# Gram stages of a two-block bottleneck network: other pixels in the first transfer step, normalisation traced step by step, issues split nine to seven

## The chip, the core and the metric

The kernel runs on one core of a Trainium2 chip, in float32. The metric is the time of one launch in device microseconds. The core has five engines that run side by side, each with its own queue of instructions, worked in order: TensorE (PE in the profile, with its weight loads as PEld), VectorE (DVE), ScalarE (ACT), GpSimd (POOL) and SyncE (SP), which here only issues transfers. Engines wait for each other through semaphores. Sixteen DMA engines move data, and a transfer is issued from the queue of one engine; in this kernel from SP, POOL and ACT.

## The reference, cut to what matters

Two residual bottleneck blocks, one after the other, each with batch normalisation over all 64 x 14 x 14 = 12,544 pixels:

```python
# x: (64, 1024, 14, 14)
out = relu(bn(conv(x, w1, b1, 1, 0), g1, be1))      # 1024 -> 256, 1x1
out = relu(bn(conv(out, w2, b2, 1, 1), g2, be2))    # 256 -> 256, 3x3
out = bn(conv(out, w3, b3, 1, 0), g3, be3)          # 256 -> 1024, 1x1
out = softplus(residual_scale)[0] * out
return relu(x + out)
# bn: (x - mean) * rsqrt(var + 1e-5), mean and var over images and pixels of each channel
```

## The kernel before

All 256 channels of the middle layer stay in on-chip memory as `y_all`: 128 partitions (channels), two halves (`MS` = 2), 12,544 pixels (`NPX`). The first convolution is fused with the last one of the block ahead; the 3x3 convolution (`conv2`) runs in a Winograd form with the products on TensorE; the last convolution is folded with its normalisation and the residual addition.

The third batch normalisation needs mean and variance of the last convolution's output before that output exists. They follow from the Gram matrix of the normalised middle activations: the sum over pixels of y yᵀ (256 x 256) and of y. Computing it is the **Gram stage** (`gram`, L904), once in each block. It goes so:

- Each piece of `y_all` is normalised in place by ScalarE (`norm`, L536, scale, shift and ReLU in one activation) and then has a constant subtracted by VectorE (`less`, L1233). Pieces are listed in `bounds`: pixels 0 to 256, to 768, to 1568, and then every 1568 (`GPX`). Both halves of each piece: 20 normalisations and 20 subtractions.
- TensorE contracts over its partitions, so pixels must lie on partitions: y has to be transposed, 256 pixels (`CH` x `P`) at a time. There are 49 such pairs of chunks. A transposed pair goes to one of six buffers `zt`, and four products (two into `g0`, two into `g1`; L169, outputs `cp` and `ap`) take it up.
- Seven of the 49 pairs are transposed by TensorE itself (`by_tensor`, L936) and copied by VectorE to `zt` (L942): the first six (`FIRST`), and the last one.
- The other 42 go through VectorE (`by_vector`, L948), whose transposition works on 32 x 32 squares. For that the squares must first be moved across partitions, by DMA: `spread(k)` (L922) moves one step of 1536 pixels (`STEP`) from `y_all` to a tile `x`, in sixteen transfers of 96 KB (L928), four by four groups of 32 partitions. There are seven steps of six pairs, with two tiles in turn (`homes`; in block 0 the first is the memory of `ws`, so the profile says `ws` and `home`; in block 1 both are `home`). Step k+2 overwrites the tile of step k, so it is issued when step k's six transpositions are done.
- The sixteen transfers of a step are issued by two queues, ten by SP and six by POOL.

Products are issued one pair behind the transpositions. After the last pair come the statistics (`conv3_stats`) and the rest of the block.

A scheduler orders the instructions of each engine when the kernel is built: it takes what was traced and picks by readiness and priority, except where `keep_in_program_order` fixes it (transpositions and products are fixed; normalisations, subtractions and copies are not). The order is then static: an engine's instruction waits for whatever stands ahead of it on that engine.

In the kernel before, all pieces are normalised and subtracted first in the trace; then two steps are spread, then the loop over pairs runs and spreads step k+2 after step k's six pairs. TensorE's first six pairs take pixels 0 to 1535; the steps take 1536 to 12,287; the last pair 12,288 to 12,543.

Of the kernel before, what the change touches and what calls it, by code (L numbers as in the profile page):

```python
# [41 lines left out]
P = 128  # L42
# [4 lines left out]
MS = M // P  # L47
# [5 lines left out]
NPX = N * HW  # L53
CH = 2
NZT = 6

FIRST, LAST = 6, 1
RUN = 3 * P
STEP = 4 * RUN
# [7 lines left out]
GPX = GI * HW  # L67
# [24 lines left out]
def bottlenecks(ctx: ExitStack, tc: tile.TileContext, x, w1s, w2s, w3s, pars, out):  # L92
    nc = tc.nc
# [5 lines left out]
    y_all = keep.tile([P, MS, NPX], FP, tag="y", name="y")  # L99
# [67 lines left out]
    def matmul(*args, **kw):  # L167

        tc.keep_in_program_order(nc.tensor.matmul(*args, **kw))  # L169
# [155 lines left out]
    def act(*args, **kw):  # L325

        tc.keep_in_program_order(nc.scalar.activation(*args, **kw))  # L327
# [205 lines left out]
    def norm(s, y, aff, act=nc.scalar.activation):  # L533

        scale, shift = aff
        act(y, y, AF.Relu, bias=shift[:, s : s + 1], scale=scale[:, s : s + 1])  # L536
# [367 lines left out]
    def gram(psum, pool, homes, aff, less, beside):  # L904

        g0, g1 = psum.tile(M + 1, "cp"), psum.tile(P + 1, "ap")
        zts = [pool.tile([P, CH, M + 1], FP, tag=f"zt{i}", name=f"zt{i}") for i in range(NZT)]
        for zt in zts:  # L910
            nc.gpsimd.memset(zt[:, :, M:], 1.0)
        zts = itertools.cycle(zts)
        start = FIRST * CH * P

        bounds = [0, CH * P, 3 * CH * P, *range(GPX, NPX + 1, GPX)]
        for a, e in zip(bounds, bounds[1:]):
            for s in range(MS):
                y = y_all[:, s, a:e]
                norm(s, y, aff)
                less(s, y)  # L920

        def spread(k):  # L922

            x = homes[k % 2][:, : MS * STEP].rearrange("p (s j f) -> p s j f", s=MS, j=4)
            for i, j in itertools.product(range(4), range(4)):
                queue = nc.gpsimd if (4 * i + j) % 8 in (2, 5, 7) else nc.sync
                a = start + k * STEP + i * RUN
                queue.dma_start(out=x[32 * i : 32 * i + 32, :, j], in_=y_all[32 * j : 32 * j + 32, :, a : a + RUN])  # L928
            return x.rearrange("p s j f -> p (s j) f")

        def by_tensor(a):
            tp = psum.tile(CH * M)
            for c in range(CH):
                for s in range(MS):
                    tc.keep_in_program_order(
                        nc.tensor.transpose(  # L936
                            tp[:, (c * MS + s) * P : (c * MS + s + 1) * P],
                            y_all[:, s, a + c * P : a + (c + 1) * P], ident,
                        )
                    )  # L940
            zt = next(zts)
            nc.vector.tensor_copy(zt[:, :, :M], tp.rearrange("p (c m) -> p c m", c=CH))  # L942
            return zt

        def by_vector(x, i):
            zt = next(zts)
            tc.keep_in_program_order(
                nc.vector.transpose(  # L948
                    zt[:, :, :M].rearrange("p b (n c) -> p b n c", c=32),
                    x[:, :, i * CH * 32 : (i + 1) * CH * 32].rearrange("p n (b r) -> p b n r", r=32),  # L950
                )
            )
            return zt

        def pairs():
            for i in range(FIRST):
                yield by_tensor(i * CH * P)
            for k in range(STEPS):
                x = ready.pop(0)
                for i in range(RUN // (CH * 32)):  # L960
                    yield by_vector(x, i)
                if k + 2 < STEPS:
                    ready.append(spread(k + 2))
            for i in range(LAST):
                yield by_tensor(NPX - (LAST - i) * CH * P)

        ready = [spread(k) for k in range(2)]
        total = NPX // (CH * P)
        before = None
        for k, zt in enumerate(itertools.chain(pairs(), (None,))):  # L970
            if before is not None:
                for c in range(CH):
                    first, last = k == 1 and c == 0, k == total and c == CH - 1
                    matmul(g0, before[:, c, 0:P], before[:, c, :], start=first, stop=last)
                    matmul(g1, before[:, c, P:M], before[:, c, P:], start=first, stop=last)
            before = zt
            if k in beside:
                beside[k]()
        return g0, g1
# [126 lines left out]
    def aggregate(stats, first):  # L1106
        n = stats.shape[1]
        mv = small.tile([P, n, nc.vector.BN_AGGR_DIM], FP, tag=f"mv{n}", name="mv")
        for o in range(n):
            nc.vector.bn_aggr(mv[:, o, :], stats[:, o, first:, :].rearrange("p t f -> p (t f)"))  # L1110
        return mv

    def affine(mv, n, par, g, be, conv_bias=None):

        def tl(name):
            return small.tile([P, n], FP, tag=f"{name}{n}", name=name)

        v, sd, r, q = tl("v"), tl("sd"), tl("r"), tl("q")  # L1120
        nc.scalar.activation(sd, mv[:, :, 1], AF.Sqrt, bias=eps)
        nc.vector.tensor_scalar(v, mv[:, :, 1], EPS, None, ALU.add)
        nc.vector.reciprocal(r, sd)

        nc.vector.tensor_mul(q, r, v)
        nc.vector.scalar_tensor_tensor(q, q, -0.5, r, ALU.mult, ALU.mult)
        nc.vector.scalar_tensor_tensor(r, q, 1.5, r, ALU.add, ALU.mult)
        scale, shift = tl("scale"), tl("shift")
        nc.vector.tensor_mul(scale, r, par[:, g : g + n])
        if conv_bias is None:  # L1130
            off = mv[:, :, 0]
        else:

            off = tl("off")
            bias = par[:, conv_bias : conv_bias + n]
            nc.vector.tensor_add(off, mv[:, :, 0], bias)
            nc.vector.tensor_sub(off, off, bias)
        nc.vector.scalar_tensor_tensor(shift, off, -1.0, scale, ALU.mult, ALU.mult)
        nc.vector.tensor_add(shift, shift, par[:, be : be + n])
        return scale, shift  # L1140
# [33 lines left out]
    with tc.tile_pool(name="first", bufs=1) as one, tc.tile_pool(  # L1174
# [17 lines left out]
        pieces = list(itertools.product(range(2), range(MS), range(MS)))  # L1192
# [16 lines left out]
    for b in range(2):  # L1209
# [4 lines left out]
        aff = affine(aggregate(stats1, T - 3 + b), MS, pb, G1, BE1)  # L1214
# [4 lines left out]
        with tc.tile_pool(name=f"last_{b}", bufs=1) as one, tc.tile_pool(  # L1219
# [5 lines left out]
            aff = affine(aggregate(stats2, 0), MS, pb, G2, BE2)  # L1225
            with ExitStack() as scope:
# [4 lines left out]
                with tc.tile_pool(name=f"gram_{b}", bufs=1) as pool:  # L1231
                    def less(k, y):
                        nc.vector.tensor_scalar(y, y, minus_c[:, k : k + 1], None, ALU.add)  # L1233

                    def x_tile(name):
                        return xpool.tile([P, CS * PX], FP, tag="x", name=name)


                    ws = sums_tile(one, 2 - b)
                    homes = [x_tile("home") if b else ws.rearrange("p i n -> p (i n)"), x_tile("home")]  # L1240

                    weights = []

                    def combined():
                        if b == 0:
                            weights.append(combine_w1(w1, ws[:, 1]))
                        weights.append(combine_w3(w3, ws[:, 0]))

                    beside = {FIRST + STEPS * RUN // (CH * 32): combined}
                    grams = gram(psum, pool, homes, aff, less, beside)  # L1250

                    made = [conv3(psum, 0, o, w3, "cx" if b else "ay") for o in range(2)]
                    mv3 = small.tile([P, CS, nc.vector.BN_AGGR_DIM], FP, tag="mv3", name="mv3")
                    conv3_stats(psum, pool, grams, w3, mv3, ("cy", "cp", "cy", "cp" if b else "cx"))
                aff = affine(mv3, CS, pb, G3, BE3, conv_bias=B3)
# [50 lines left out]
```

## Time and profile before

| | us |
|---|---|
| median of seven runs | 2016.35 (2015.07 to 2018.89) |
| the profiled execution: its time / its span | 2015.07 / 2013.1 |
| block 0, first normalisation of the Gram stage starts | 603.98 |
| block 0, first VectorE transposition starts | 626.90 |
| block 0, TensorE's first products for the statistics, behind the Gram products | 690.25 |
| block 1, first normalisation starts | 1597.51 |
| block 1, first VectorE transposition starts | 1620.34 |
| granted TensorE clock, mean over the span | 0.985 |

One profiled execution lies behind the profile; its time includes some 2 us that are not in the span. A line of the waits reads: engine, line, what it waited for, then total us, times, longest. A line of the timeline reads: start, us, engine, line, operation, output and input with shapes, how many, and in brackets the idle time before with what ended it. A line of windows reads: stretch, its length, then busy us (and instructions) of PE, PEld, DVE, ACT and POOL, the granted TensorE clock as a share of full speed, the DMA engines' share and GB/s. For a group of instructions: busy us and mean ns of one behind the bar.

### The profile page before, as it was taken

Reading aid. Unit: us, or ns where it says so; the run is one execution under the profiler, and the core shown is the slowest. Engines: PE = TensorE matmul, PEld = TensorE weight load, DVE = VectorE, ACT = ScalarE, POOL = GpSimd, SP = SyncE. Lnnn points to the kernel's source line nnn. Section 1 sums busy time; section 2 is a strip of 40 time slices with the busy share of each in tenths; the row PEclk is TensorE's granted clock in tenths of the full one; section 3 lists DMA queues with packets and bytes.
Section 4 is the critical chain, followed back from the end, with each engine's and each line's share of the span. In section 5 each row is a group of like instructions: output and inputs, shape, how many; then the busy total and the mean of one; then the engine's idle time right before and its main releaser. Section 6 shows DMA issues by size and latency. Waiting matters only on the chain.

```text
span 2013.1 us, 27547 instructions
## 1 busy us (share of the span) xinstructions
PE 1947.4 (97%) x9560; PEld 1641.1 (82%) x9560; DVE 1586.8 (79%) x2844; ACT 940.5 (47%) x1915; POOL 617.0 (31%) x676
## 2 busy tenths in 40 slices
PE   8999999999987999999999999999999888999999
PEld 4555558999987889999999999899999876555554
DVE  5788758999986566777777677699999864899897
ACT  1222214466645055555555555445566521556555
POOL 0111101121213134333333433211221140666665
PEclk9999999999998999999999999999999898999999
DMA  7866625555546534444444444256656384799998
GB/s 269 291 249 248 247 97 175 181 191 186 190 136 179 199 128 161 176 178 166 187 161 184 169 170 183 96 181 191 194 184 193 100 203 172 259 327 334 329 338 299
DMA packets 176218, 407.63 MB, mean 202 GB/s; under 512 B 12368, under 2 KB 143504, under 8 KB 159568
## 3 DMA queue, kind: packets, MB, share of 16 engines
q1 hardware_dynamic: 162208, 330.44, 48.1%
q10 hardware_dynamic: 5328, 50.86, 6.1%
q0 software_dynamic: 8544, 24.59, 3.7%
q8 instruction: 75, 1.23, 0.2%
q14 instruction: 63, 0.52, 0.1%
HBM read 267.95 MB, written 115.87 MB: 191 GB/s over the span
## 4 chain that ended last, share of the span: by engine, by line
PE 80%; DVE 11%; DMA 5%; issue 1%; ACT 1%; POOL 1%; SPq 0%; DVEq 0%; ACTq 0%; POOLq 0%
PE ay L169 16%; PE cy L169 13%; PE cp L169 11%; PE ap L169 10%; PE odd L169 6%; PE even L169 6%; PE m L169 5%; PE ax L169 5%; PE l L169 4%; PE cx L169 4%; DMA x<-mid 2%; DMA out<-x 2%; DVE x L453 1%; PE ps L169 1%; DVE sums L589 1%
## 5 line engine op out<-in xcount | busy, mean ns | idle before, releaser
L327 ACT ACTIVATE cu<-cy,scale 128x196 f32<-128x196 f32 (+1 forms) x552 | 256.9, 474 | 298.7 <-PE cy L169 291.4
L592 POOL TENSOR_TENSOR diffs<-r 128x448 f32<-128x448 f32 (+1 forms) x80 | 112.2, 1414 | 507.9 <-DVE r L574 265.7
L453 DVE SCALAR_TENSOR_TENSOR x<-cp,scale,x 128x196 f32<-128x196 f32 (+1 forms) x368 | 178.0, 484 | 83.9 <-PE cp L169 81.0
L327 ACT ACTIVATE x<-x,shift 128x392 f32<-128x392 f32 x368 | 211.5, 614 | 69.0 <-POOL x L479 53.1
L169 PE MATMUL cy<-ct,ws 128*128 128x196 f32 (+1 forms) x736 | 221.7, 383 | 2.5 <-ACT cu L327 2.5
L474 POOL TENSOR_TENSOR x<-x,cu 128x196 f32<-128x196 f32 (+1 forms) x184 | 167.4, 910 | 171.1 <-ACT cu L327 170.8
L169 PE MATMUL ay<-at,ws 128*128 128x196 f32 (+1 forms) x752 | 209.3, 381 | 1.0 <-ACT au L327 1.0
L479 POOL TENSOR_TENSOR x<-x,cu 128x392 f32<-128x392 f32 x124 | 125.9, 1015 | 191.2 <-DVE x L453 186.5
L169 PEld LDWEIGHTS ay<-at,ws 128*128 128x128 f32 x752 | 136.3, 190 | 35.1 <-ACT au L327 1.9
L169 PEld LDWEIGHTS cy<-ct,ws 128*128 128x128 f32 x736 | 133.6, 190 | 36.9 <-ACT cu L327 3.8
L500 POOL TENSOR_TENSOR x<-x,cu 128x392 f32<-128x392 f32 x120 | 125.0, 1042 | 84.1 <-DVE x L453 77.8
L169 PE MATMUL m<-sums,ua 128*128 128x224 f32 (+1 forms) x752 | 145.5, 336 | 0.0
L169 PE MATMUL cp<-zt 128*128 128x257 f32 x392 | 122.8, 396 | 15.3 <-DVE zt L948 15.3
L169 PE MATMUL cx<-y,w 128*128 128x196 f32 (+1 forms) x412 | 129.7, 402 | 5.0 <-DVE x L1025 5.0
L169 PEld LDWEIGHTS m<-sums,ua 128*128 128x128 f32 x752 | 131.3, 189 | 0.2
L453 DVE SCALAR_TENSOR_TENSOR x<-cx,scale,x 128x196 f32<-128x196 f32 (+1 forms) x184 | 89.1, 484 | 51.7 <-PE cx L169 51.4
L169 PE MATMUL cy<-y,w 128*128 128x196 f32 (+1 forms) x404 | 126.3, 399 | 0.0
L169 PE MATMUL even<-v,ub 128*128 128x224 f32 (+1 forms) x640 | 123.8, 334 | 0.8 <-ACT even L686 0.8
L169 PE MATMUL odd<-v,ub 128*128 128x224 f32 (+1 forms) x640 | 123.8, 335 | 0.2
L169 PE MATMUL l<-diffs,ub 128*128 128x224 f32 (+1 forms) x640 | 122.0, 333 | 0.0
L327 ACT ACTIVATE au<-ay 128x196 f32<-128x196 f32 (+1 forms) x141 | 53.6, 380 | 139.7 <-PE ay L169 139.0
L169 PE MATMUL cp<-y,ws 128*128 128x196 f32 (+1 forms) x368 | 113.8, 391 | 4.3 <-DVE x L453 2.9
(211 smaller groups left out, 4339.7 us busy)
## 6 DMA issues: line engine op xcount, KB each, us to landing
x<-in_x SPq DMA_DIRECT2D x62, 1568.0 KB, 6.8
ub<-u SPq DMA_DIRECT2D x80, 768.0 KB, 4.8
x<-mid SPq DMA_DIRECT2D x32, 1568.0 KB, 9.9
mid<-x ACTq DMA_DIRECT2D x31, 1568.0 KB, 5.1
out<-x SPq DMA_DIRECT2D x124, 392.0 KB, 6.7
ua<-u SPq DMA_DIRECT2D x96, 256.0 KB, 3.1
ub<-u SPq DMA_DIRECT2D x16, 1024.0 KB, 6.0
u<-y POOLq DMA_DIRECT2D x40, 256.0 KB, 6.3
```

Of the source, the lines that this page charges most:

```text
L169: tc.keep_in_program_order(nc.tensor.matmul(*args, **kw))
L327: tc.keep_in_program_order(nc.scalar.activation(*args, **kw))
L453: nc.vector.scalar_tensor_tensor(v, bank, self.scale[:, o : o + 1], v, ALU.mult, ALU.add)
L474: nc.gpsimd.tensor_add(self.part(1, 1), self.part(1, 1), u3)
L479: nc.gpsimd.tensor_add(v, v, self.u12)
L500: nc.gpsimd.tensor_add(v, v, self.u12[:, i * self.n : (i + 1) * self.n])
L589: nc.vector.tensor_add(sums, r[:, :, :, WH:], r[:, :, :, :WH])
L592: nc.gpsimd.tensor_sub(diffs, r[:, :, :, :WH], r[:, :, :, WH:])
```

## The change

Three edits, all in `gram`:

1. TensorE's six first pairs are no longer the first 1536 pixels. It takes three pairs from pixels 0 to 767, then three from 2304 to 3071; the first step of transfers takes the pixels between, 768 to 2303 (`head` = 768). Later steps are as before.
2. The pieces are cut to match: 256, 512, 1536, 832, and then 1568 each. They are no longer all traced at the start, but by `norm_to`, as far as the step to be spread needs them; what is left is traced ahead of the last pair.
3. Of the sixteen transfers of a step, POOL issues seven and SP nine.

```diff
+        head = FIRST // 2 * CH * P
         start = FIRST * CH * P
-
-        bounds = [0, CH * P, 3 * CH * P, *range(GPX, NPX + 1, GPX)]
-        for a, e in zip(bounds, bounds[1:]):
-            for s in range(MS):
-                y = y_all[:, s, a:e]
-                norm(s, y, aff)
-                less(s, y)
+        bounds = [0, CH * P, head, head + STEP, *range(2 * GPX, NPX + 1, GPX)]
+        pieces = list(zip(bounds, bounds[1:]))
+
+        def norm_to(end):
+
+            while pieces and pieces[0][0] < end:
+                a, e = pieces.pop(0)
+                for s in range(MS):
+                    y = y_all[:, s, a:e]
+                    norm(s, y, aff)
+                    less(s, y)

         def spread(k):

+            first = start + k * STEP if k else head
+            norm_to(first + STEP)
             x = homes[k % 2][:, : MS * STEP].rearrange("p (s j f) -> p s j f", s=MS, j=4)
             for i, j in itertools.product(range(4), range(4)):
-                queue = nc.gpsimd if (4 * i + j) % 8 in (2, 5, 7) else nc.sync
-                a = start + k * STEP + i * RUN
+                queue = nc.gpsimd if 4 * i + j in (1, 3, 6, 8, 10, 13, 15) else nc.sync
+                a = first + i * RUN
                 queue.dma_start(out=x[32 * i : 32 * i + 32, :, j], in_=y_all[32 * j : 32 * j + 32, :, a : a + RUN])
...
         def pairs():
             for i in range(FIRST):
-                yield by_tensor(i * CH * P)
+                a = i * CH * P
+                yield by_tensor(a if a < head else a + STEP)
             for k in range(STEPS):
...
+            norm_to(NPX)
             for i in range(LAST):
                 yield by_tensor(NPX - (LAST - i) * CH * P)
```

In the instruction order of the two built kernels, the Gram stages apart, nothing differs. In them TensorE, ScalarE and GpSimd keep their orders apart from the new shapes and the seven issues in place of six; on VectorE the subtractions stand elsewhere among copies and transpositions.

## The prediction

> **What bounds the kernel now.** I read the busy table and the forty slices first, then the waits around the first Gram stage, then VectorE's order in time there. A Gram stage runs twice, at 601 to 690 us (block 0) and 1594 to 1680 us (block 1).
>
> ```profile
> span 2013.1 us, 27547 instructions
> PE 1947.4 (97%) x9560; PEld 1641.1 (82%) x9560; DVE 1586.8 (79%) x2844; ACT 940.5 (47%) x1915; POOL 617.0 (31%) x676
> PE   8999999999987999999999999999999888999999
> ```
>
> TensorE is busy for 97% of the span; the few slices with 7 or 8 are the places where time can be had, and two lie at the Gram stages. The waits between 600 and 690 us name the hole there, and a window says what follows it (its columns are busy us of PE, PEld, DVE, ACT and POOL):
>
> ```profile
> PE cp L169 <- DVE zt L948: 8.4, 1, 8.4
> ```
>
> ```profile
> 627.00:690.25 63.25, 62.51 (x358) 55.35 (x358) 35.38 (x58) 3.85 (x4) 15.78 (x30) 0.97 0.75 234
> ```
>
> TensorE stands 8.4 us once, until VectorE's first 32x32 transposition (L948) gives it a pair of chunks; after 627 us it is busy 62.51 of 63.25 us, so from there its own work sets the stage's end. In block 1 the wait is 6.9 us, until 1620.34 + 0.75 = 1621.09. Whatever brings that first transposition forward brings the end of the stage forward, microsecond for microsecond. What holds it is in VectorE's order:
>
> ```profile
> 611.92 1.97 DVE L1233 TENSOR_SCALAR y<-y,minus_c 128x1568 f32<-128x1568 f32 x2
> ...
> 617.49 3.05 DVE L1233 TENSOR_SCALAR y<-y,minus_c 128x1568 f32<-128x1568 f32 x3
> 621.10 1.04 DVE L1233 TENSOR_SCALAR y<-y,minus_c 128x1568 f32<-128x1568 f32 x1 [0.55 <-ACT y L536]
> 622.68 1.04 DVE L1233 TENSOR_SCALAR y<-y,minus_c 128x1568 f32<-128x1568 f32 x1 [0.55 <-ACT y L536]
> 624.27 1.03 DVE L1233 TENSOR_SCALAR y<-y,minus_c 128x1568 f32<-128x1568 f32 x1 [0.55 <-ACT y L536]
> 625.85 1.04 DVE L1233 TENSOR_SCALAR y<-y,minus_c 128x1568 f32<-128x1568 f32 x1 [0.55 <-ACT y L536]
> 626.90 1.31 DVE L948 STREAM_TRANSPOSE zt<-ws 128x512 f32<-128x512 f32 x2
> ```
>
> Before the transposition stand seven subtractions in a row (L1233), the last four 1.583 us apart, each waiting for ScalarE's normalisation (L536). So ScalarE's pace sets 626.90. Block 1 is alike: the last subtraction starts at 1619.38, the transposition at 1620.34. The transfers it reads were there by then:
>
> ```profile
> 613.92 8.07 SPq L928 DMA_DIRECT2D ws<-y  x10
> 614.19 5.38 POOL L928 DMA_DIRECT2D ws<-y  x6 [12.92 <-DVE y L1233]
> ```
>
> The tenth issue on SP's queue starts near 621.34 and, by the issue table of that stretch, lands some 3.8 us on, at about 625.1; POOL's sixth starts at 618.62 and lands 4.8 us on, at 623.4. Slack against 626.90: 1.8 us.
>
> **The change part by part.** Units: ScalarE's normalisations by shape.
>
> ```profile
> L536 ACT ACTIVATE y<-y,shift,scale 128x1568 f32<-128x1568 f32 x14 | 22.3, 1685 | 0.0
> L536 ACT ACTIVATE y<-y,shift,scale 128x800 f32<-128x800 f32 x2 | 2.0, 1040 | 0.0
> L536 ACT ACTIVATE y<-y,shift,scale 128x512 f32<-128x512 f32 x2 | 1.5, 800 | 0.0
> L536 ACT ACTIVATE y<-y,shift,scale 128x256 f32<-128x256 f32 x2 | 1.1, 594 | 1.4 <-DVE shift L1139 1.4
> ```
>
> Consecutive ones overlap by 0.10 us (1.685 against the 1.583 cadence), so they advance by 0.49, 0.70, 0.94 and 1.583 us, and between the last two shapes by 0.277 + 0.000833 us per pixel: 1.557 for the new 1536, 0.970 for the new 832. Two of each: 5.05 us, as before (2 x 0.94 + 2 x 1.583 = 5.05). Twenty normalisations and twenty subtractions remain; the pieces alone cost nothing.
>
> The order is the point. In the built order of the new kernel, seven of the twelve 1568-pixel subtractions precede the first transposition (before: eleven of fourteen), five follow the sixth transposition in a block. ScalarE work ahead of the first transposition, after the common 256s and 512s: before 2 x 0.94 + 11 x 1.583 = 19.29 us; after 5.05 + 7 x 1.583 = 16.13. Difference 3.16 us in each block: 626.90 becomes 623.74, 1620.34 becomes 1617.18.
>
> Will the transfers be there? The first step now needs pixels 768 to 2303, so both 1536 subtractions. ScalarE gives these at 607.92 and 609.47; VectorE does the first by 609.0, the copy of chunk 1 (0.65), the second by 610.75. So the issues start 3.2 us earlier than 613.92, and in block 1, where the second one ends at 1604.3, 3.8 us before 1608.10. SP issues nine, one slot (about 0.7 us) less. Landing: 625.1 - 3.2 - 0.7 = 621.2, ahead of 623.74 by 2.5 us. POOL's seventh adds one of its 0.95 us slots: 623.4 - 3.2 + 0.95 = 621.2 too.
>
> TensorE's chunks 3 to 5 move to pixels 2304 to 3071 and wait for the 832 subtractions, at 613.2 instead of a start at 612.42. Chunk by chunk (1.31 us of matmuls, 0.6 of transposes, 0.65 of copy) they end near 620.7 instead of 619.3; the pause before 624.5 hides that. In block 1 the clock's slow start already puts chunk 3 at 1607.4, so nothing moves. The second step needs the subtractions up to pixel 4703, done near 617.2 as before; its issues follow SP's ninth and land by about 628.
>
> Then the five subtractions: six transpositions from 623.74 end at 627.4 (3.68 for six), five subtractions at 0.99 end at 632.4 (ScalarE's last ends at 630.5), and the second step's first pair is ready at 633.15. TensorE, started at 624.5, needs six pairs: before, 627.67 to 637.1, so 633.9 now. Cover 0.75 us; without it the price is that same fraction of a microsecond. The third step overwrites the first tile after 627.4 instead of 633.42, so later steps gain room. There the TensorE queue has no wait on transpositions already, so nine-to-seven, which shortens SP's 7.2 us per step to 6.5, is worth nothing beyond the start.
>
> Clock. After the pause TensorE runs at half clock for about 3.3 us:
>
> ```profile
> 623.00:626.00 3.00, 0.00 (x0) 0.00 (x0) 1.90 (x3) 3.00 (x3) 1.35 (x2) 0.68 0.97 255
> 626.00:631.00 5.00, 3.33 (x10) 2.86 (x11) 4.99 (x7) 4.58 (x3) 0.00 (x0) 0.51 0.52 137
> ```
>
> The granted clock falls 2.1 to 5.2 us after TensorE stops (worked out from the granted clock of short windows over the four pauses at 598, 619, 1591 and 1614 us). New pauses: 3.7 us, in the middle of that. If the clock still falls, the slow start costs what it costs now; if not, 1.6 us more is won per stage, less the 0.75 of cover that is then gone. I take the fall: 0, bounds -0.9 and +0.9 per stage.
>
> Sum: -3.16 - 3.16 = **-6.3 us**. The profiled execution took 2015.07 us (span 2013.1 and 2.0 around it): it would take 2008.8. The median lies 1.28 higher, so 2016.35 - 6.3 = **2010.0 us**. What follows a Gram stage (statistics, residual, the fused and the last stage) starts from its end and from queues that move with it.
>
> A rule against the change. The trace's price of a POOL issue is 0.95 us while VectorE subtracts (5.38 for six, dearest 1.35) and 0.53 when VectorE is quiet. The Trainium skill, "SBUF — State Buffer", section "A bandwidth-pool intuition that's wrong (but worth ruling out)", says that a GpSimd-issued DMA is held up while VectorE has the shared port, and gives about 3100 ns for one that takes 620 alone. By that figure seven issues would take an estimated 21.7 us, end at 632.5 and make each stage some 10 us longer; the trace has the direction and a third of the size.
>
> **The rivals.**
> 1. One stage does not move, or both move by half: -3.2 us, 2013.2. For it: the chain of waits puts a transfer of the second tile (issued 623.81, 3.09 us) right before the transposition at 626.90, so landing could be what counts. Against: that transposition reads only the first tile, whose last issue lands at 625.1, and transfers start 3 us earlier too. It would need a first step that takes 16 us from issue to landing; it took 11.2.
> 2. POOL's queue becomes the last to land: slower. Place: the seven issues from 610.95 while VectorE subtracts and copies. They are late from (623.74 - 4.8 - 610.95) / 7 = 1.14 us each, and the kernel turns slower than before from 1.6 us each. At twice the mean, 1.9 us: 610.95 + 13.3 + 4.8 = 629.1, 2.15 us later than before in each block, +4.3, 2020.7. For it: the dearest issue, 1.35. Against: the mean of six is 0.90 to 0.95, and in block 1 twelve take 10.57, 0.88 each.
> 3. The clock stays up through the shorter pause: a further -1.8 us over both stages, 2008.2. Against: the pause at 598 us lost it after 2.1 us.
> 4. The earlier end is lost in the last stage, where the transfer engines are 90 to 96% busy: up to +6.3, 2016.35. Against: these engines are 18% busy at 1680 to 1700, so the stage starts from an empty queue and moves as a whole.
>
> **How the numbers follow.** Forecast 0.72, rival 1 0.12, rival 2 0.05, rival 3 0.08, rival 4 0.03. A measurement of this kernel can tell about 0.2%, 4 us, from no change. Faster by more than that: forecast and rival 3, 0.80. Within it: rivals 1 and 4, 0.15. Slower: 0.05. The likeliest case alone spans 2008 to 2012 (clock bounds and the scatter of 2015.07 to 2018.89). The range for 8 in 10 goes from rival 3 with the low end of that scatter, 2006.8, to rival 1, 2013.6.
>
> **What would show it.** First transposition 19.7 us after the first normalisation (22.9 and 22.8 now); TensorE's one wait on L948 near 4 us, not 8.4 and 6.9; no wait there afterwards; subtractions in a block of five after the sixth transposition; POOL issues under 1.1 us. The forecast is wrong if the first transposition's wait ends on a transfer, if TensorE stands again before the second step's pairs, or if the stages after 690 us grow longer.

## The result

| | before | after |
|---|---|---|
| median, us | 2015.86 of 35 runs (2010.37 to 2021.73) | 2010.09 of 14 runs (2003.70 to 2012.96) |
| ratio to before | | 0.9968, 95% interval 0.9960 to 0.9976 |
| profiled execution, time / span, us | 2015.07 / 2013.1 | 2010.48 / 2008.7 |
| granted TensorE clock, mean | 0.985 | 0.985 |
| first VectorE transposition after first normalisation, block 0 / 1, us | 22.92 / 22.83 | 19.81 / 19.65 |

The changed kernel is faster by 0.32%, 5.8 us between the medians; 2010.0 was forecast. The page of the changed kernel begins so:

```profile
span 2008.7 us, 27547 instructions
PE 1950.8 (97%) x9560; PEld 1644.0 (82%) x9560; DVE 1588.6 (79%) x2844; ACT 940.0 (47%) x1915; POOL 626.0 (31%) x690
PE   8999999999988999999999999999999898999998
```

The busy shares say nothing: 97% as before, over a span 4.4 us shorter. The difference is in TensorE's waits for VectorE's transpositions at the two Gram stages (engine, line, what it waited for, then total us, times, longest; block 0, then block 1):

```profile
PE cp L169 <- DVE zt L956: 3.5, 1, 3.5
...
PE cp L169 <- DVE zt L956: 3.3, 1, 3.3
```

They were 8.4 and 6.9. TensorE still waits once in each stage for the first transposition, but for less. VectorE's order in block 0 of the changed kernel (start, us, engine, line, operation, shapes, how many):

```profile
617.46 2.92 DVE L1243 TENSOR_SCALAR y<-y,minus_c 128x1568 f32<-128x1568 f32 x3
620.91 1.04 DVE L1243 TENSOR_SCALAR y<-y,minus_c 128x1568 f32<-128x1568 f32 x1 [0.53 <-ACT y L536]
622.02 3.68 DVE L956 STREAM_TRANSPOSE zt<-ws 128x512 f32<-128x512 f32 x6
625.63 4.78 DVE L1243 TENSOR_SCALAR y<-y,minus_c 128x1568 f32<-128x1568 f32 x5
...
631.20 3.68 DVE L956 STREAM_TRANSPOSE zt<-home 128x512 f32<-128x512 f32 x6 [0.59 <-DMA ws<-y]
```

Only one subtraction now waits for ScalarE just ahead of the transpositions, where before there were four in a row. The six transpositions stand together, and the five other subtractions come behind them in one block. The issues of transfers in the same kernel, SP's and then POOL's queue:

```profile
608.91 6.86 SPq L936 DMA_DIRECT2D ws<-y  x9
...
625.73 5.76 SPq L936 DMA_DIRECT2D ws<-y  x9
...
609.18 3.95 POOL L936 DMA_DIRECT2D ws<-y  x7 [9.68 <-DVE y L1243]
```

The first step's transfers start 5.0 us earlier than before (613.92), of which 1.77 is an earlier start of the whole stage (first normalisation 602.21 against 603.98). The third step, which overwrites the first tile, is issued at 625.73, as soon as the sixth transposition has read that tile. That line turns out to matter as much as the first transposition.

**Where the 4.4 us of the two profiled executions lie.** Stage by stage, after minus before: up to block 0's first normalisation -1.77; from it to the first transposition -3.11; from there to the statistics products -0.14; from these to the residual +2.09; up to block 1's first normalisation -0.72; to its first transposition -3.18; from there to the statistics +1.44; to the residual +1.76; last stage -0.76. So 6.3 us come where they were forecast, 5.3 us go in the stretches behind the transpositions, and 3.4 us come elsewhere. All three losses lie where the granted clock falls.

The loss of 1.44 us is in block 1's Gram stage. By the clock record of the trace, TensorE's clock is at half for 6.83 us there in both kernels, from 1617.38 before and from 1613.48 after. TensorE comes back from its pause at 1621.09 before, with 3.1 us of these left, and at 1614.27 after, with 6.0 us left. Windows (PE, PEld, DVE, ACT, POOL busy, granted clock, DMA share, GB/s) of the kernel before,

```profile
1621.00:1624.00 3.00, 2.91 (x9) 2.53 (x10) 3.00 (x5) 3.00 (x2) 0.00 (x0) 0.50 0.94 186
1624.00:1627.00 3.00, 3.00 (x19) 2.71 (x18) 3.00 (x6) 0.10 (x1) 0.00 (x0) 0.96 0.03 5
```

and of the changed one:

```profile
1614.00:1617.00 3.00, 2.73 (x8) 2.36 (x9) 3.00 (x6) 3.00 (x3) 0.00 (x0) 0.50 0.88 159
1617.00:1621.00 4.00, 4.00 (x15) 3.46 (x15) 4.00 (x6) 3.45 (x3) 0.59 (x1) 0.59 0.34 79
```

The products of one chunk follow each other at 0.66 us when the clock is up. The first three took 3.6 us before, the first five 6.3 us after: 1.6 and 3.0 us lost to the clock. In block 0 the same reckoning gives 1.7 and 1.8 us.

The losses of 2.09 and 1.76 us are in the statistics, in 48 one-column products. In block 1 these take 7.4 us, and 5.6 in the kernel before. For block 0 the chain of work that ended last shows it (start, us, what):

```profile
694.81 5.92 PE ax L169 x48
```

is the kernel before,

```profile
689.79 8.02 PE ax L169 x48
```

the changed one: the same 48 products, 2.1 us longer. Windows of 3 us say why. Before, the clock is still high in the third microsecond of these products:

```profile
694.00:697.00 3.00, 3.00 (x24) 2.54 (x23) 1.68 (x3) 0.00 (x0) 0.00 (x0) 1.00 0.00 0
697.00:700.00 3.00, 3.00 (x26) 3.00 (x25) 0.00 (x0) 0.00 (x0) 0.00 (x0) 0.87 0.00 0
```

After, it is down:

```profile
691.00:694.00 3.00, 3.00 (x20) 3.00 (x20) 0.25 (x1) 0.00 (x0) 0.00 (x0) 0.65 0.00 0
694.00:697.00 3.00, 3.00 (x15) 3.00 (x16) 0.00 (x0) 0.00 (x0) 0.00 (x0) 0.50 0.00 0
```

In both the clock falls while these products run, at 699.2 before and at 691.9 after, so a different number of them meets half clock. The same changed kernel, profiled once more (again_after below), spends 5.77 us on them, so this is no price of the edit. Nor is the 1.77 us ahead of block 0 a gain of it: the kernel before has 6.83 us at half clock from 313.5 us on, the first profile of the changed kernel has none there, and again_after has them again and starts block 0's first normalisation at 604.26.

### The profile page after: what moved, and what is told of

It is laid out like the page before. It is cut to its first block, busy times and chain, and to the rows that moved or that the text cites. A ratio compares the mean times of both kernels' runs of the same rounds, so it can differ in the third digit from the quotient of the medians.

```text
span 2008.7 us, 27547 instructions
## 1 busy us (share of the span) xinstructions
PE 1950.8 (97%) x9560; PEld 1644.0 (82%) x9560; DVE 1588.6 (79%) x2844; ACT 940.0 (47%) x1915; POOL 626.0 (31%) x690
## 4 chain that ended last, share of the span: by engine, by line
PE 80%; DVE 10%; DMA 7%; issue 1%; ACT 1%; POOL 0%; SPq 0%; DVEq 0%; ACTq 0%; POOLq 0%
PE ay L169 16%; PE cy L169 12%; PE cp L169 10%; PE ap L169 10%; PE even L169 6%; PE odd L169 6%; PE m L169 5%; PE ax L169 5%; PE l L169 4%; PE cx L169 4%; DMA x<-mid 4%; DMA out<-x 2%; DVE x L453 1%; PE ps L169 1%; DVE r L574 1%
```

## The experiments

All ratios are to the kernel before, run on the same chip in the same rounds. Each edit is one of the change's parts alone or undone, or an addition that singles out a cause.

### The pixels alone, the split alone, the tracing alone, and the change without the split

**swap_only**: edit 1 with all pieces traced at the start, ten and six issues.

```diff
+        bounds = [0, CH * P, head, head + STEP, *range(2 * GPX, NPX + 1, GPX)]
...
+            first = start + k * STEP if k else head
...
-                yield by_tensor(i * CH * P)
+                a = i * CH * P
+                yield by_tensor(a if a < head else a + STEP)
...
+        norm_to(NPX)
         ready = [spread(k) for k in range(2)]
```

> Only the pixels change places (first edit, with its pieces): all pieces are traced at the start as before, the issues stay ten to six. Theory ORDER (what sets the first transposition is ScalarE's pace over the subtractions that stand ahead of it on VectorE): seven of the twelve long ones stand ahead, as in the changed kernel, so the first transposition comes 19.7 us after the first normalisation in both stages (before: 22.9 and 22.8), -3.2 us a stage, -6.3 us in all. Rival LANDING (the transfers' landing sets it): the transfers start 3.2 and 3.8 us earlier, so -3.2 and -3.8 as well, but with the last landing right at the transposition. Rival SPLIT (nine to seven is what counts): no change.

**split_only**: edit 3 alone, `queue = nc.gpsimd if 4 * i + j in (1, 3, 6, 8, 10, 13, 15) else nc.sync`.

> Only the issues change, nine to seven; pixels and tracing as before. The scheduler then puts ten of fourteen long subtractions ahead of the first transposition instead of eleven. ORDER: one normalisation less, 1.58 us, so first transposition 21.3 us after the first normalisation, -1.6 us a stage, -3.2 us in all. LANDING: one SP slot of 0.7 us less, -0.7 us a stage, -1.4 us in all. SPLIT: the whole -6.3 us.

**trace_only**: edit 2 with the old pieces, old pixels and ten and six issues.

```diff
+            norm_to(first + STEP)
...
                     ready.append(spread(k + 2))
+            norm_to(NPX)
```

> Only the tracing changes: pieces as before, normalised and subtracted in the trace as far as a step needs them; pixels and issues as before. Eleven long subtractions still stand ahead of the first transposition, three follow the sixth in a block instead of one between each. ORDER: first transposition at 22.9 us as before, 0 us in all (between -0.5 and +0.5). Rival TRACE (tracing step by step is what brings the transpositions forward): -3 us a stage.

**no_split**: the changed kernel with ten and six issues.

> The changed kernel with the issues put back to ten and six. Same order of VectorE as the changed kernel. ORDER: first transposition at 19.7 us, time as the changed kernel, -6.3 us against before. LANDING: the tenth SP issue lands 0.7 us later, so 0.7 us a stage slower than the changed kernel, -4.9 us. SPLIT: no faster than before.

| | median us | ratio, 95% interval | first transposition, block 0 / 1 | TensorE's waits for it, us (times), block 0; block 1 |
|---|---|---|---|---|
| before | 2015.86 | | 22.92 / 22.83 | 8.4 (1); 6.9 (1) |
| swap_only | 2015.60 | 1.0 [0.9991, 1.0008] | 19.74 / 19.65 | 7.0 (2); 5.4 (2) |
| split_only | 2016.66 | 1.0 [0.9991, 1.001] | 22.90 / 21.24 | 9.8 (2); 6.8 (2) |
| trace_only | 2014.95 | 0.9993 [0.9984, 1.0002] | 22.92 / 22.81 | 8.3 (1); 7.9 (1) |
| no_split | 2009.03 | 0.9964 [0.9951, 0.9976] | 19.76 / 19.65 | 4.4 (2); 3.3 (1) |

None of the three edits alone makes a difference that can be measured. The pixels and the tracing together make all of it, and the split adds nothing: no_split's interval covers the changed kernel's.

swap_only is the instructive one. The first transposition comes as early as in the changed kernel, 19.7 us, and nothing is won. VectorE's order in its block 0:

```profile
623.22 0.72 DVE L955 STREAM_TRANSPOSE zt<-ws 128x512 f32<-128x512 f32 x1
623.86 1.00 DVE L1242 TENSOR_SCALAR y<-y,minus_c 128x1568 f32<-128x1568 f32 x1
624.77 0.71 DVE L955 STREAM_TRANSPOSE zt<-ws 128x512 f32<-128x512 f32 x1
...
631.06 0.71 DVE L955 STREAM_TRANSPOSE zt<-ws 128x512 f32<-128x512 f32 x1
...
644.10 3.68 DVE L955 STREAM_TRANSPOSE zt<-ws 128x512 f32<-128x512 f32 x6 [8.55 <-DMA home<-y]
```

Between each two transpositions stands a subtraction, so that six transpositions take from 623.22 to 631.77, 8.55 us instead of 3.68. Only then is the first tile free, and SP issues the third step:

```profile
631.79 8.07 SPq L935 DMA_DIRECT2D ws<-y  x10
```

It can be transposed at 644.10, 40.62 us after the first normalisation. In the kernel before that was 644.48 - 603.98 = 40.50, the same, though the first transposition was 3.2 us later. TensorE, which starts on the twelve pairs of two steps at 623.99 and is through at 641.28, stands for the third step (start, us, operation, in brackets the idle time):

```profile
644.87 0.70 PE L169 MATMUL cp<-zt 128*128 128x257 f32 x2 [3.58 <-DVE zt L955]
```

The same twelve pairs started at 627.67 in the kernel before and lasted until 645.1, by the starts of their products; the third step's first pair was ready at 644.48 + 0.65 = 645.1. That kernel had two limits of the same height: the first transposition, and the third step's landing, which came just as TensorE ran out of pairs. Edit 1 lowers the first alone. That the twelve pairs take some 17.4 us in both is chance. At full clock and without a wait they would take 15.8; before, the first products ran at half clock (1.7 us), while in swap_only the clock stays at 1.00 through the pause, and the first six pairs take 9.25 us instead of 7.9 because their transpositions come 1.6 us apart. In the changed kernel the third step is transposed from 635.94, 33.7 us after the first normalisation: the tracing of edit 2 made the scheduler put the five subtractions behind the six transpositions, and that lowers the second. trace_only does put a block there (three subtractions), but leaves eleven ahead, and the first limit stays.

The split in the kernel before is a small loss in block 0. POOL's issues of the first step in split_only, and the transposition that waits for them:

```profile
614.38 6.33 POOL L928 DMA_DIRECT2D ws<-y  x7 [13.07 <-DVE y L1233]
```

```profile
626.92 1.31 DVE L948 STREAM_TRANSPOSE zt<-ws 128x512 f32<-128x512 f32 x2 [1.58 <-DMA home<-y]
```

Seven issues at 0.90 us each end at 620.71, and a transfer holds the transposition for 1.58 us; a subtraction fewer stands ahead of it there, which makes up for that. In the changed kernel the same seven issues take 3.95 us, 0.56 each: VectorE subtracts for 1.21 of these 3.95 us, and did for 4.09 of the 5.38 in which POOL issued six in the kernel before (0.90 each). It is the subtractions that count, and not only how busy VectorE is. In swap_only VectorE is busy for the whole of six issues, but with transpositions, and they take 0.53 each:

```profile
632.06:635.23 3.17, 3.17 (x21) 2.90 (x21) 3.17 (x6) 0.00 (x0) 3.17 (x6) 1.00 0.60 145
```

### The same kernel again

**again_after** is the changed kernel, profiled and timed once more.

> The changed kernel once more, unedited, for a second profile of it. Theory ORDER: first transposition 19.7 us after the first normalisation again (19.8 and 19.6 in its first profile). Theory CLOCK (what the first profile gave back, 4 us beside the Gram stages' heads, is where the granted clock falls): the 48 one-column products of the statistics (8.0 and 7.2 us there, 5.9 and 5.5 before) and the slow stretch after the pause (3.5 and 5.9 us) change from execution to execution with no edit, each within what the two profiles so far span. Rival: they are properties of the changed kernel and come out as in its first profile, within 0.2 us.

2010.35 us, ratio 0.9975 [0.9963, 0.9986], first transposition 19.81 / 19.70, waits 4.1 and 3.2. Between this and the first profile of the changed kernel, the stretch of block 0 from VectorE's first operation on the finished Gram matrix to its first copy of the statistics took 10.64 and 12.89 us, with no edit between them; in the kernel before it took 10.80. So a difference of 2.09 us there needs no edit. In block 1 the stretch took 13.98 and 14.03 (12.28 before), but 14.83 in split_only, which has the old pixels, and 12.17 in swap_3tiles below, which has the new ones: it follows none of the three edits. What sets the moment of the clock's fall was not singled out, nor why the two profiles of the changed kernel agree in block 1. They agree there in the Gram stage too: again_after loses 3.1 us to the clock behind the pause (3.0 in the first profile, 1.6 in the kernel before).

### A third tile for the pixels alone

If swap_only loses its gain because the third step has to wait for the first tile, then a third tile must give the gain back, with the subtractions left between the transpositions. The edit against swap_only:

```diff
-            x = homes[k % 2][:, : MS * STEP]...
+            x = homes[k % 3][:, : MS * STEP]...
...
-                    homes = [x_tile("home") if b else ws..., x_tile("home")]
+                    homes = [x_tile("home") if b else ws..., x_tile("home"), x_tile("home")]
```

> Edit 1 alone as in swap_only (10 and 6 issues, all pieces traced ahead), but with three tiles in turn, so that the third step of transfers needs no tile to come free. VectorE keeps swap_only's order: seven long subtractions ahead of the first transposition, then one between each two. Theory (swap alone gives its gain back because its six transpositions, stretched over 7.9 us by the subtractions between them, free the first tile at 631.8 and the third step lands too late): first transposition still 19.7 us after the first normalisation in both blocks, the wait of 8.55 us of VectorE on the third step's transfers at about 636 to 644 us gone, TensorE waits on the transposition once in each block, about 3.6 to 3.9 us; time below swap_only's 2015.6 by the second waits of 3.4 and 1.5 us, 2009.5 to 2011.5. Rival (the interleaved subtractions slow TensorE's pairs themselves, or the granted clock takes the gain back): the second wait goes, or stays under another name, and the time stays at 2014 to 2017. The third tile is one that the loads of x would have had: the first loads behind the stage can start later, which is read from the stages after it.

2008.51 us, ratio 0.9967 [0.9955, 0.9978], a microsecond under the range expected; why it is that much better was not singled out. The first transposition is where it was (19.75 / 19.66), TensorE waits once in each block (3.5 and 3.9), and the wait of 8.55 us is gone; VectorE's timeline of block 0:

```profile
630.77 0.71 DVE L955 STREAM_TRANSPOSE zt<-ws 128x512 f32<-128x512 f32 x1
...
631.59 4.90 DVE L955 STREAM_TRANSPOSE zt<-home 128x512 f32<-128x512 f32 x8
637.09 0.71 DVE L955 STREAM_TRANSPOSE zt<-home 128x512 f32<-128x512 f32 x1 [0.60 <-PE ap L169]
```

The eight are the second step's six and two of the third, without a pause; from 637.09 VectorE waits for TensorE. The third tile is taken from the loads of x, but nothing behind the stage is later for it: block 0's residual starts 97.2 us after the first normalisation, in swap_only 101.2. So the tile that comes free late is what cost swap_only its gain. The subtractions in between are not free: the first six pairs take 9.24 us here too, against 8.0 in no_split, where the six transpositions stand together and the clock is up as well. These 1.3 us in block 0 do not undo the gain.

### Subtractions in program order

In the changed kernel VectorE still does seven of the 1568-pixel subtractions ahead of the first transposition, though the first two steps of transfers need only two of them (pixels up to 4607). The order was the scheduler's. **order** is the changed kernel with the subtractions kept where they are traced:

```diff
-                        nc.vector.tensor_scalar(y, y, minus_c[:, k : k + 1], None, ALU.add)
+                        tc.keep_in_program_order(
+                            nc.vector.tensor_scalar(y, y, minus_c[:, k : k + 1], None, ALU.add)
+                        )
```

> The changed kernel with the subtractions kept in the order of the trace: two long ones ahead of the first transposition instead of seven, then two after each step's six transpositions. ORDER: the first transposition is free of ScalarE and comes when the copies of TensorE's chunks are done and the transfers have landed, some 16 us after the first normalisation; TensorE's pause of 3.5 us shrinks to under 0.5, so the clock has no reason to fall: -3.3 for the pause and -1.6 for the slow start in each stage, some -9.8 us against the changed kernel, about 2000 us. Rival LANDING: no gain, the first transposition stays at 19.7. Rival LATER (the two subtractions between steps hold up the next step's transfers until TensorE stands): the pause goes, but waits come back at later steps, and the gain is under 5 us.

**order_no_split** is the same with ten and six issues.

> As the run before, with ten issues on SP and six on POOL. With the subtractions out of the way the landing decides, so here the split should show if anywhere: ORDER plus a landing that is now last: 0.7 us a stage slower than with nine to seven. Rival: transfers are limited by the DMA engines, which are over 90% busy then, not by the queue: no difference (under 0.3 us a stage).

**order_no_swap** has the subtractions kept in order and the pieces traced step by step, but the pixels and pieces of the kernel before, and ten and six issues.

> Subtractions kept in program order as in the run named order and pieces traced step by step (edit 2), but without the other pixels in the first step (edit 1 undone) and with 10 and 6 issues. Four long subtractions and both 800s stand ahead of the first transposition, as much work for ScalarE as in order. What is left is the transfer: the first step needs pixels up to 3071, which VectorE gives at about 613.9, and takes 9.5 to 11.2 us from its first issue to its landing (order_no_split and before). Theory (pixels and order are two separate bounds, and the later of them decides): first transposition 19.4 to 21.1 us after the first normalisation, waiting on a transfer, TensorE waits 4.9 to 6.6 us for it in each block; against order_no_split's 2001.4 later by 3.1 to 4.9 us in each block and by about 1.6 us each for the clock lost in the pause: 2010 to 2014.5. Rival (once the order is fixed the change of pixels is worth nothing): first transposition near 16.3 us, no pause, time 2000 to 2003.5.

| | median us | ratio, 95% interval | first transposition, block 0 / 1 | TensorE's wait, block 0; block 1 | clock |
|---|---|---|---|---|---|
| order | 1997.64 | 0.9911 [0.9896, 0.9926] | 16.12 / 15.74 | 0.4; 0.2 | 0.990 |
| order_no_split | 2001.43 | 0.9923 [0.9908, 0.9938] | 16.27 / 15.77 | 0.5; 0.3 | 0.989 |
| order_no_swap | 2015.36 | 1.0003 [0.9992, 1.0015] | 24.44 / 22.50 | 9.8; 7.9 | 0.983 |

**order beats both kernels.** VectorE in its block 0:

```profile
619.66 3.68 DVE L956 STREAM_TRANSPOSE zt<-ws 128x512 f32<-128x512 f32 x6 [1.49 <-DMA home<-y]
623.26 1.94 DVE L1244 TENSOR_SCALAR y<-y,minus_c 128x1568 f32<-128x1568 f32 x2
627.32 3.68 DVE L956 STREAM_TRANSPOSE zt<-home 128x512 f32<-128x512 f32 x6 [2.12 <-DMA ws<-y]
```

Two subtractions follow each step's six transpositions, and the transposition now waits for a transfer (1.49 us) instead of ScalarE. TensorE hardly stands there any more (0.4 and 0.2 us), and the gain, 12.7 us to again_after in the same rounds, is larger than the two pauses (4.1 and 3.2). The products behind them ran at half clock for a while, which cost again_after a further 1.6 and 3.1 us; together that makes 11.4 of the 12.7 us. The granted clock over 621 to 641 us was 0.91 in the changed kernel, and here it is 1.00 (window, its length, PE, PEld, DVE, ACT, POOL, clock, DMA share, GB/s):

```profile
621.00:641.00 20.00, 20.00 (x124) 18.36 (x123) 15.29 (x22) 9.15 (x6) 8.03 (x16) 1.00 0.78 210
```

Nine and seven against ten and six makes 0.15 us at the first transposition in block 0 and 0.03 in block 1; the two times cannot be told apart.

order_no_swap says what the pixels are worth once the order is right: all of it. It missed the range expected (19.4 to 21.1 us for the first transposition, up to 2014.5 us) on the slow side. Its issues, SP's and then POOL's, and the transposition:

```profile
615.05 8.32 SPq L936 DMA_DIRECT2D ws<-y  x10
...
615.32 4.47 POOL L936 DMA_DIRECT2D ws<-y  x6 [13.08 <-DVE y L1244]
619.78 3.15 POOL L936 DMA_DIRECT2D home<-y  x6
```

```profile
629.39 3.68 DVE L956 STREAM_TRANSPOSE zt<-ws 128x512 f32<-128x512 f32 x6 [10.68 <-DMA home<-y]
```

The first step's issues start 10.1 us after the first normalisation, 3.4 us later than in order_no_split (610.36 there), and by then the second step's are ready too: POOL issues the second step's six at 619.78 while SP is still at the first step's ten. The transfer engines carry both at once (218 to 246 GB/s at a full share from 620 to 628 us), and 14.3 us pass from the first issue to the transposition, against 9.6 in order_no_split. The expectation had priced the transfer by runs in which the two steps came more one after the other.

### Twelve issues on POOL

**order_pool12** is order with twelve of each step's sixteen issues on POOL and four on SP, to price POOL's issues.

> As the ordered kernel, with twelve issues on POOL and four on SP, to price POOL's queue where the landing decides. At 0.56 us an issue (seven in 3.95 us in the changed kernel) POOL ends 0.5 us after SP's nine did: under 1 us a stage slower than the ordered kernel. At the 0.95 us of the kernel before: twelve in 11.4, 5 us a stage slower. By a price of about 3.1 us an issue: 37 us, 30 us a stage slower.

2044.01 us, ratio 1.0143 [1.0126, 1.016]; first transposition 17.96 / 18.20. POOL's queue and SP's in block 0:

```profile
611.65 7.94 POOL L936 DMA_DIRECT2D ws<-y  x12 [9.68 <-DVE y L1244]
...
629.13 0.53 POOL L936 DMA_DIRECT2D home<-y  x1 [3.63 <-DMA home<-y]
```

```profile
621.21 2.66 SPq L127 DMA_DIRECT2D x<-in_x  x3
```

Twelve issues take 7.94 us, 0.66 each, and the first transposition comes 1.8 and 2.5 us later than in order. The rest of the loss of 46 us must lie elsewhere; the queues show that SP, with four issues a step, reaches three loads of x (1568 KB each) before the third step, and that POOL's issues, one by one, wait for transfers to land (15.1 us in ten waits). VectorE then stands 19.3 us for the second step. The two are mixed in the time, so it is no price of an issue; the 7.94 us are.

## Why the prediction was right, point by point

- **What bounds the stage.** Right: the count of long subtractions ahead of the first transposition, at ScalarE's pace. -3.16 us forecast for each block, -3.11 and -3.18 measured, and the offset 19.8 and 19.65 against 19.7. order shows the same cause from the other side: with two long ones ahead the transposition comes 3.7 and 3.9 us earlier still.
- **Transfers in time.** Right, with more slack than forecast. SP's ninth issue starts at 615.18 and lands 2.7 us on, at 617.9, 4.1 us ahead of the transposition (forecast 2.5). POOL's issues cost 0.56 us, not 0.95: VectorE subtracts less while they run. The figure of the Trainium skill that the prediction weighed, about 3100 ns beside a VectorE copy for a GpSimd-issued transfer that takes about 620 ns alone ("SBUF — State Buffer", "A bandwidth-pool intuition that's wrong (but worth ruling out)"), was met by POOL's issues in no run: their groups in the Gram stages have means from 0.53 to 0.90 us, and the dearest single one took 1.35. The direction is the skill's, the size less than a third. (From the prediction's own 610.95 its 21.7 us end at 632.65, not at 632.5.)
- **The block of five.** Right in place; the second step's first pair is ready at 631.9 us, where the forecast's 633.15, less the stage's earlier start of 1.77, gave 631.4, and TensorE, which takes this pair up at 632.45, has no wait there. The cover was 0.5 us against 0.75, and it held with the help of the slow clock behind the pause. In no_split the clock stayed up in block 0, TensorE was through its six pairs sooner, and it waited 0.96 us for the second step.
- **The clock.** In block 0 of the changed kernel the fall after the pause came as taken (0.70 over 622 to 626 us), and the slow start cost what it cost before (1.8 against 1.7 us). In block 1 it was mis-sized: the slow start cost 3.0 us against 1.6, so 1.4 us came back, outside the bound of 0.9 per stage. again_after shows the same. That all behind the stage would move as a whole did not hold in the single execution either. The stages behind the transpositions differ by up to 2.1 us either way, and after 690 us block 0's stretch grew by that, one of the prediction's own signs of being wrong; again_after had it at its old length. With 6.3 us from the transpositions and 1.4 back, 4.9 us would be left. The medians, 5.8 us apart, and the ratio, 0.32% or 6.5 us with an interval from 4.8 to 8.1, cannot tell 4.9 from 6.3.
- **The issues, nine to seven.** Worth nothing, as forecast (no_split, order_no_split).
- **The term that was mis-sized.** "The third step overwrites the first tile after 627.4 instead of 633.42, so later steps gain room" stood there with no price. The runs give it one: without it, swap_only, the whole gain goes. The sum was right because both parts were in the change, and in that it was lucky: it put the whole gain down to the first transposition. The statement that from 627 us on TensorE's "own work sets the stage's end" was wrong. It was busy for 62.51 of 63.25 us since the third step arrived just then, not since nothing else limited it.
- **The rivals.** None came in the two profiles of the changed kernel. A landing that decides (the first) and POOL as last to land (the second) need first transpositions that wait for transfers; these do in order_no_swap and order_pool12 (10.68 and 3.93 us) and, for less, in split_only and order (1.58 and 1.49). The clock kept up through the pause (the third) is not far off: in block 0 of swap_only, no_split and swap_3tiles it stayed at 1.00 over 620 to 632 us through pauses of 3.45, 3.46 and 3.45 us, and fell in the changed kernel's two profiles with 3.55 and 4.10 us (0.86 over the same stretch in each). The last stage gave nothing back (the fourth): it was 0.76 us shorter.

## What to carry to other kernels

An engine that is busy all through a stretch may be fed just in time there: before counting a gain at the stretch's start microsecond for microsecond, take the time at which each later batch is ready and subtract when it will then be needed. With two buffers in turn, what stands between the reads of the first buffer on the reading engine decides when the third batch can start, and a third buffer or a better order does the same there. Where a scheduler places independent work, read its built order ahead of the first critical instruction, and pin it if it puts more there than that instruction needs: here that was worth twice the change itself.

## What the runs showed of the hardware

- The granted clock changes on a grid: the slow stretches in the clock records of the traces last 3.41 us or a multiple of it (6.83, 10.24, 13.65, 17.07), but for the one cut off by the end of the run. Without that one it is 61.4 us at half clock in the kernel before, 58.0 and 61.4 in two profiles of the changed one, and 41.0 in order.
- A pause of TensorE of some 3.5 us cost the clock in some executions (3.55 us, first profile of the changed kernel) and not in others (3.45 us, swap_only). What a shorter pause saves can come back in part, when more of the same slow stretch then falls on work: 6.0 us against 3.1 in block 1.
- It falls in the middle of work, too: in the 48 one-column products of the statistics, with TensorE busy for 3.00 of 3.00 us. In two executions of the changed kernel it did so 2.1 and 4.5 us into these products.
- What a POOL issue costs goes with VectorE's subtractions (float32, in place): 0.53 us with none of them, though VectorE was busy all the time with 32x32 transpositions (swap_only); 0.56 with subtractions for 31% of the time (changed kernel); 0.90 with 76% (kernel before).
- With two steps of sixteen 96 KB transfers whose data are ready together, the first of them took 4.8 us more from its first issue to the transposition (order_no_swap 14.3, order_no_split 9.6), though each queue issues them in order. The one comparison differs in the pixels too; it was not singled out.
